# Layer 1's first projections moved into the last batch of layer 0, in a kernel of two attention layers

## The chip, the cores and the metric

The kernel runs on one core of a Trainium2 chip. The metric is the device time of one execution in microseconds (us), the median of several runs; lower is better. PE is the core's matrix engine, DVE its vector engine, ACT its scalar engine, SP the engine whose queue issues nearly all DMAs here, and PSUM the small memory that PE writes its products to. SBUF is the larger memory in which tiles live, on 128 partitions.

## The reference

Two attention layers run one after the other over x of 8 batches, 512 channels and 32x32 = 1024 tokens, in float32. The parts that matter, shortened:

```python
def _gn(v, G=32, eps=1e-5):        # group norm: 16 channels x 1024 tokens to a group
    ...
x = x + _L0_conv_ref(_gn(x), ...)  # layer 0
x = x + _L1_conv_ref(_gn(x), ...)  # layer 1

# layer 0: a second group norm, then 8 heads of 64 channels
qkv = einsum('oc,bct->bot', qkv_w, normed) + qkv_b
weight = softmax(einsum('bct,bcs->bts', q, k))
a = einsum('bts,bcs->bct', weight, v)
out = einsum('oc,bct->bot', proj_w, xf + a) + proj_b

# layer 1: heads are mixed by an 8x8 matrix before the softmax, normed over a head's whole map after it
attn = einsum('bhdq,bhdT->bhqT', q, k) * scale
attn = softmax(einsum('gh,bhqT->bgqT', w_head, attn))
attn = (attn - mean) / sqrt(var + EPS) * in_gamma + in_beta   # per batch and head
out = einsum('bhqT,bhdT->bhqd', attn, v).reshape(b, t, c) @ w_proj.T + b_proj
```

Layer 1 of batch 0 needs layer 0 of batch 0 alone. Nothing in it needs layer 0 of batch 7.

## The kernel before, in words

The order of the instructions on each engine is the order of the program, written by hand. All eight batches go through layer 0 (`with ExitStack() as l0`, from L650), then all eight through layer 1 (`l1`, from L1149). x after layer 0 is written to DRAM (`x1_d`) and read again by layer 1. Each layer opens its own pools of SBUF and PSUM, so layer 1's tiles lie where layer 0's were.

**A projection** of 512x512 weights over 1024 tokens is made by seven products of half-size blocks in place of eight (a Strassen-Winograd scheme). Its left factors are seven combinations of the weights' blocks, kept in DRAM and loaded as one tile of 1.75 MB (`load_left`); its right factors are four differences of the activations' blocks, made on DVE (`combine_right`, tiles `tmp` in layer 0). In layer 0 `project0` (L860) issues the products through `product` (L856) and calls `finish` as each quarter of the output is complete; in layer 1 the class `Projection` does it in the order of `ORDER` (L1297), and `leave` takes a product out of PSUM. The order matters in that the quarter finished last frees its PSUM, and becomes readable, last. The left tiles of layer 0 have two buffers in turn (`wpool`), so a load waits for the projection two before it.

**Layer 0.** `attention0(b, agenda)` runs 64 steps i over (half of the tokens f, pair of heads hp, block of 128 keys kc), two at a time: `scores` (L982) on PE, exp on ACT (L987), and two steps later `values` (L1008) on PE and `sums` on DVE (L993, L995), which add up the exponentials in `zacc`. Eight steps make a group g. Two steps after a group, `totals` adds `zacc` over the partitions on PE by a matrix of ones (L1030, tile z), ACT and DVE copy a half of the result each (L1035, L1036), and two small DMAs bring one line of each into 128 rows (`zc`). Four steps on, `reciprocals` adds the halves of `values` on DVE, inverts zc, writes it to DRAM and reads it back spread over the partitions (`zd`, `rzb`; L1049, L1052). Four steps after that, `finish` multiplies and adds into `xa` on DVE (L1068, L1070).

An `Agenda` holds work to be issued at a given step. In all batches but the last, the next batch's statistics (`stats0`: pm at L620 at slot 43, pv at L631 at slot 45), the loads of its left factors and its normalization (slots 49 to 61) are on it, and after the attention the next batch's k is projected, then the rest of the agenda runs (the last group's totals, reciprocals and finish), then v, q, and the batch's own output projection `out0`. In the last batch nothing follows: the agenda runs, then `out0`, then `stats_out` (L646, L647) for the four channel blocks.

**Between the layers.** All group statistics of layer 1 are finished for all batches at once (`GroupStats`: `means`, `squares`, `root`; pm L620, pv L631, then some 20 small DVE instructions), y of batch 0 is loaded (L1251) and normalized (L1273, L1277), and k, half of v, the sums of v (L1411) and q of batch 0 are projected. wv is loaded into the second buffer of `re_t`.

**Layer 1.** `Attention1.half_step(x)` runs for 32 half steps and five more. Each makes two blocks of scores (L1575), which DVE or ACT copy into `raw` (L1588, L1590); every second half step a tile t of `raw` is complete and eight DMAs of 256 KB regroup it, one for each r, into a buffer of `re_t` (L1599), at first all at once (x up to `MLAG` = 4), later one behind each score or mix. Four half steps later `mix` (L1623) reads it, with the exponential on ACT, the sums and sums of squares on DVE, and `values` (L1669) one half step after. A mix is 64 small products and needs all eight r. `pieces` are further DMAs, one issued behind each block of scores from x = 5 on: the next batch's y and left factors of k, and, put ahead of these three times a batch, rzb, the inverse of the sums. The second half of v (`v_pair`, L1394) is made at x = 1 and x = 2; its weights lie in the first half of the buffer of `re_t` that tile t = 1 is regrouped into.

Of the kernel before, what the change touches and what calls it, by code (L numbers as in the profile page):

```python
# [18 lines left out]
P = 128  # L19
# [448 lines left out]
def tile_two_attention_layers(  # L468
# [25 lines left out]
    FB = 512  # L494
# [109 lines left out]
    class GroupStats:  # L604
# [8 lines left out]
        def tile(self, tag, bufs=None):  # L613
            return self.pool.tile([P, self.w], F32, tag=tag, name=f"{tag}_{self.nm}", bufs=bufs)
# [27 lines left out]
    def channel_stats(pool, x, mv, nm):  # L642
# [4 lines left out]
        nc.vector.bn_aggr(mv, bn.rearrange("p f s -> p (f s)"))  # L647


    with ExitStack() as l0:  # L650
# [157 lines left out]
        def normalize0(b, c):  # L808
            if c == 0:
                n_t[b] = act.tile([P, NCC, T], F32, tag="n", name=f"n_{b}")  # L810
# [89 lines left out]
        def qk0(b, which):  # L900
            tiles, o0 = (q_t, 0) if which == "q" else (k_t, 1)
            t = tiles[b] = act.tile([P, NCC, T], F32, tag=which, name=f"{which}0_{b}")
# [15 lines left out]
        def v0(b):  # L918
            t = v_t[b] = act.tile([P, NT, C], F32, tag="v", name=f"v0_{b}")
# [20 lines left out]
            project0(f"pv0_{b}", "v", n_t[b], finish, by_token=True)  # L940

# [28 lines left out]
        def attention0(b, agenda):  # L970
# [50 lines left out]
            def totals(g):  # L1021

                z = [
                    ps_a.tile([P, FB], F32, tag="a0", name=f"z_{b}_{g}", bufs=2),
                    small_psum(f"z_{b}_{g}_1"),
                ]
                for a in range(2):
                    rows = slice(a * D, a * D + D)
                    for m in range(2):
                        nc.tensor.matmul(  # L1030
                            z[a][m * D : m * D + D], ones[rows, :D], zacc[g][rows, m],
                            start=True, stop=True,
                        )
                row = zpool.tile([P, 2, FB], F32, tag="row", name=f"row0_{b}_{g}", bufs=1)
                nc.scalar.copy(row[:, 0], z[0])  # L1035
                nc.vector.tensor_copy(row[:, 1], z[1])  # L1036
                zc[g] = stat.tile([P, 2, T // P], F32, tag="zc", name=f"zc_{b}_{g}")
                for a in range(2):
                    nc.sync.dma_start(out=zc[g][:, a], in_=row[0::D, a])

            def reciprocals(g):

                nc.vector.tensor_add(u[g][0], u[g][0], u[g][1])
                zs = stat.tile([P, T // P], F32, tag="zs", name=f"zs_{b}_{g}")
                nc.vector.tensor_add(zs, zc[g][:, 0], zc[g][:, 1])
# [60 lines left out]
        for b in range(B):  # L1106
# [22 lines left out]
            else:  # L1129
                ag.at(32, lambda: load_left("p", b))  # L1130
            attention0(b, ag)
            slot = NI + 2
            if more:
                combine_right(f"{b + 1}", n_t[b + 1])
                qk0(b + 1, "k")
            ag.flush()
# [845 lines left out]
```

## Time and profile before

| What | us |
|---|---|
| median of 3 runs (4342.40 to 4345.67) | 4345.27 |
| the profiled execution, its own time | 4355.81 |
| its span, first to last instruction | 4353.9 |
| layer 0's last attention ends on PE | 1747.2 |
| first scores of layer 1 | 1869.6 |
| first scores of layer 1's second batch | 2185.5 |
| PE busy | 4192.3 |
| DVE busy | 2911.7 |
| ACT busy | 2329.9 |
| mean granted clock of PE | 0.995 |

Busy time is the union of an engine's instructions; matmuls are pipelined, so a busy PE is not PE at its peak. In a line of the timeline the numbers are the start, the length, the engine, the line of the program, the operation, what it writes and reads, the shape and the count of instructions merged; idle time ahead of it stands in brackets with what ended it. One product of float32 in the program is two matmul instructions in the trace.

### The profile page before, as it was taken

Reading aid. Unit: us, or ns where it says so; the run is one execution under the profiler, and the core shown is the slowest. Engines: PE = TensorE matmul, PEld = TensorE weight load, DVE = VectorE, ACT = ScalarE, POOL = GpSimd, SP = SyncE. Lnnn points to the kernel's source line nnn. Section 1 sums busy time; section 2 is a strip of 40 time slices with the busy share of each in tenths; the row PEclk is TensorE's granted clock in tenths of the full one; section 3 lists DMA queues with packets and bytes.
Section 4 is the critical chain, followed back from the end, with each engine's and each line's share of the span. In section 5 each row is a group of like instructions: output and inputs, shape, how many; then the busy total and the mean of one; then the engine's idle time right before and its main releaser. Section 6 shows DMA issues by size and latency. Waiting matters only on the chain.

```text
span 4353.9 us, 131477 instructions
## 1 busy us (share of the span) xinstructions
PE 4192.3 (96%) x58568; PEld 2243.2 (52%) x58568; DVE 2911.7 (67%) x3881; ACT 2329.9 (54%) x2730; POOL 53.3 (1%) x86
## 2 busy tenths in 40 slices
PE   7999999999999999799999999999999999999998
PEld 4353535353535353356466466466466466465565
DVE  4748484848484848458668668568577578577577
ACT  1717171717171716158368278277187287286385
POOL 0000000000000000000000000000000000000000
PEclk9999999999999999899999999999999999999999
DMA  4213131212121211257367377277286286375474
GB/s 145 77 54 101 50 104 49 79 49 79 52 76 54 74 49 43 87 140 191 123 166 183 105 187 180 97 195 189 81 202 172 90 206 158 114 199 141 135 175 136
DMA packets 260464, 521.21 MB, mean 120 GB/s; under 512 B 58992, under 2 KB 66544, under 8 KB 253232
## 3 DMA queue, kind: packets, MB, share of 16 engines
q1 hardware_dynamic: 255008, 509.92, 41.8%
q8 instruction: 461, 7.55, 0.8%
q0 software_dynamic: 2576, 0.69, 0.3%
q10 hardware_dynamic: 2304, 2.10, 0.2%
q14 instruction: 115, 0.94, 0.1%
HBM read 196.11 MB, written 46.92 MB: 56 GB/s over the span
## 4 chain that ended last, share of the span: by engine, by line
PE 84%; DVE 6%; DMA 5%; ACT 2%; issue 2%; SPq 1%; POOL 0%; DVEq 0%; ACTq 0%; POOLq 0%
PE a L1669 11%; PE s L1575 11%; PE m L1623 10%; PE s L982 8%; PE a L1008 8%; PE pk L1319 5%; PE pq L1319 4%; PE pp_p L856 4%; PE pv_p L856 4%; PE pv L1394 4%; PE pk_p L856 4%; PE pq_p L856 4%; PE pp L1319 3%; DMA re<-raw 2%; PE t L1700 2%
## 5 line engine op out<-in xcount | busy, mean ns | idle before, releaser
L1623 PEld LDWEIGHTS m<-wmix,re 64*64 64x64 f32 x32768 | 585.4, 135 | 141.9 <-issue 73.7
L1623 PE MATMUL m<-wmix,re 64*64 64x64 f32 x32768 | 602.1, 219 | 44.0 <-issue 34.9
L987 ACT ACTIVATE e<-s 128x1024 f32<-128x1024 f32 x512 | 497.4, 1026 | 235.4 <-PE s L982 235.4
L1629 ACT ACTIVATE e<-m 128x1024 f32<-128x1024 f32 x512 | 528.2, 1032 | 157.7 <-PE m L1623 154.2
L1647 DVE TENSOR_TENSOR z<-z,e 128x1024 f32<-128x1024 f32 x448 | 538.9, 1218 | 69.8 <-ACT e L1629 69.6
L1651 DVE TENSOR_TENSOR z<-z,e 128x1024 f32<-128x1024 f32 x448 | 534.9, 1219 | 74.6 <-ACT e L1640 74.4
L1669 PE MATMUL a<-e,v 128*64 128x256 f32 x4096 | 558.2, 392 | 27.5 <-ACT q L1691 20.9
L1575 PE MATMUL s<-k,q 64*64 64x256 f32 x8192 | 558.4, 388 | 6.2 <-DVE q L1431 4.6
L1590 ACT COPY raw<-s 128x1024 f32<-128x1024 f32 x368 | 372.7, 1015 | 284.4 <-PE s L1575 245.8
L982 PE MATMUL s<-q,k 64*64 64x512 f32 x4096 | 491.5, 594 | 2.3 <-ACT e L987 2.3
L995 DVE TENSOR_TENSOR zacc<-zacc,e 128x1024 f32<-128x1024 f32 x384 | 468.2, 1219 | 28.6 <-ACT e L987 3.9
L1008 PE MATMUL a<-e,v 64*64 64x512 f32 x4096 | 485.0, 589 | 0.0
L1640 ACT ACTIVATE e<-e 128x1024 f32<-128x1024 f32 x448 | 462.1, 1063 | 0.0
L1575 PEld LDWEIGHTS s<-k,q 64*64 64x64 f32 x8192 | 271.5, 132 | 274.5 <-issue 170.7
L1669 PEld LDWEIGHTS a<-e,v 128*64 128x64 f32 x4096 | 250.6, 136 | 155.0 <-issue 24.9
L1008 PEld LDWEIGHTS a<-e,v 64*64 64x64 f32 x4096 | 159.9, 133 | 281.2 <-issue 281.2
L982 PEld LDWEIGHTS s<-q,k 64*64 64x64 f32 x4096 | 156.2, 133 | 281.5 <-issue 257.7
L1588 DVE COPY raw<-s 128x1024 f32<-128x1024 f32 x144 | 176.1, 1223 | 96.3 <-PE s L1575 84.7
L1394 PE MATMUL pv<-re,y 128*128 128x512 f32 x512 | 227.6, 598 | 0.0
L1394 PEld LDWEIGHTS pv<-re,y 128*128 128x128 f32 x512 | 94.8, 190 | 120.1 <-issue 120.1
L1399 DVE COPY v<-pv 128x512 f32<-128x512 f32 x32 | 22.1, 689 | 149.4 <-ACT v L1398 149.4
L856 PE MATMUL pv_p<-left_v,tmp 128*128 128x256 f32 x512 | 115.1, 383 | 4.2 <-DVE tmp L885 4.2
(285 smaller groups left out, 4133.0 us busy)
## 6 DMA issues: line engine op xcount, KB each, us to landing
re<-raw SPq DMA_DIRECT2D x1024, 256.0 KB
left_q<-left_q SPq DMA_DIRECT2D x17, 1792.0 KB
left_p<-left_p SPq DMA_DIRECT2D x17, 1792.0 KB
left_k<-left_k SPq DMA_DIRECT2D x10, 1792.0 KB
x<-in_x_dram SPq DMA_DIRECT2D x32, 512.0 KB
rzb<-zd SPq DMA_DIRECT2D x128, 128.0 KB
x<-x SPq DMA_DIRECT2D x64, 256.0 KB
rzb<-zd SPq DMA_DIRECT2D x64, 256.0 KB
```

The costliest lines, as they stand in the source:

```text
L856: nc.tensor.matmul(out, st, mv, start=start, stop=(k == 1), skip_group_check=True)
L982: nc.tensor.matmul(ps[c * D : c * D + D, m], k[r, hp, k0 : k0 + D], q[r, hp, ts(f, FB)], start=True, stop=True,)
L987: nc.scalar.activation(e[i], ps, AF.Exp, scale=S0 * S0)
L1008: nc.tensor.matmul(acc[g][a][m * D : m * D + D], v[rows, kc, ts(2 * hp + m, D)], e[i][rows, m], start=(kc == 0), stop=(kc == NG - 1),)
L1319: nc.tensor.matmul(self.ps[m][:, i], w[:, left, k * HC + i * P : k * HC + i * P + P], right[:, k], start=(k == 0 and m != 2), stop=(k == 1 ...
L1394: nc.tensor.matmul(ps[:, m], y_t[b][:, c, ts(2 * i + m, P)], w[:, c], start=(c == 0), stop=(c == NCC - 1),)
L1575: last = nc.tensor.matmul(pv[c * D : c * D + D, m, j], qo_t[b][r, 2 * qb + j, hp, ts(c, D)], k_t[b][r, hp, ts(kb, KB)], start=True, stop=True,
L1623: last = nc.tensor.matmul(ps[c * D : c * D + D, a, ts(r, D)], self.re[t, r][rows, j, k0 : k0 + D], wmix[rows].rearrange("p g i -> p (g i)" ...
L1629: nc.scalar.activation(self.e[y][:, j], ps.rearrange("p a c -> p (a c)"), AF.Exp)
L1647: nc.vector.tensor_add(self.z[:, j], self.z[:, j], self.e[y][:, j])
L1651: nc.vector.tensor_add(self.z2[:, j], self.z2[:, j], self.e2[j])
L1669: last = nc.tensor.matmul(self.acc[w][two * D : two * D + D, s].rearrange("p (c i) -> p c i", i=Q8), v_t[b][:, kc, ts(g, D)], e[:, g], sta ...
```

## The change

Six things are changed. (1) The tiles n, q, k and v of both layers come from one pool, `shared`, that stays open over both. (2) In layer 0's last batch, y of layer 1's batch 0 is loaded at slot 20, the group statistics of batches 0 to 6 are finished at slots 22, 25 and 28, the left factors of layer 1's k and q are loaded at 32 and 33 (before: those of `out0` at 32), and y is normalized at 49 to 61; after the attention come layer 1's k, the rest of the agenda, the load for `out0`, layer 1's q, the load of wv, `out0`, and then the first two pairs of v with `stats_out` between them. These use layer 0's `project0`. (3) In layer 1's first batch the statistics of batch 7 alone are finished at half steps 0, 1 and 2. (4) `totals` makes one z in four products of 128 rows, 32 columns of ones and 256 elements, ACT alone copies it, and one DMA makes zc; the addition of two halves on DVE is gone. (5) `ORDER` ends with 3, 4 for 4, 3. (6) The second v pair of a layer 1 batch is made in half step 3, after its scores and mix and ahead of its regrouping; tile t = 1 is regrouped in the order 4 to 7, 0 to 3; and rzb is spread by four DMAs of 32 partitions in place of two of 64.

```diff
+    shared = both.enter_context(tc.tile_pool(name="shared", bufs=1))
+    gstat = both.enter_context(tc.tile_pool(name="gstat", bufs=1))
+    def group_stages(b0, b1, psum):
+        gs = GroupStats(
+            gstat, psum, mvs[:, b0:b1].rearrange("p b c s -> p (b c) s"), f"1_{b0}", keep=1
+        )
+        def end():
+            gs.root()
+            at = slice(b0 * NCC, b1 * NCC)
+            nc.vector.tensor_copy(gmean[:, at], gs.gm)
+            nc.vector.tensor_copy(grstd[:, at], gs.r1)
+            nc.vector.scalar_tensor_tensor(
+                gneg[:, at], gs.gm, -1.0, gs.r1, ALU.mult, ALU.mult
+            )
+            nc.vector.scalar_tensor_tensor(
+                ys[:, b0:b1].rearrange("p b c -> p (b c)"), gs.dm, float(T), gs.r1,
+                ALU.mult, ALU.mult,
+            )
+        return gs.means, gs.squares, end
+    def normalize_to(y, b, c):
+        i = b * NCC + c
+        if c % 2:
+            nc.scalar.activation(
+                y, y, AF.Identity, bias=gneg[:, i : i + 1], scale=grstd[:, i : i + 1]
+            )
+        else:
+            nc.vector.tensor_scalar(
+                y, y, gmean[:, i : i + 1], grstd[:, i : i + 1], ALU.subtract, ALU.mult
+            )
...
-                n_t[b] = act.tile([P, NCC, T], F32, tag="n", name=f"n_{b}")
+                n_t[b] = shared.tile([P, NCC, T], F32, tag="n", name=f"n_{b}")
...
-            t = tiles[b] = act.tile([P, NCC, T], F32, tag=which, name=f"{which}0_{b}")
+            t = tiles[b] = shared.tile([P, NCC, T], F32, tag=which, name=f"{which}0_{b}")
...
-            t = v_t[b] = act.tile([P, NT, C], F32, tag="v", name=f"v0_{b}")
+            t = v_t[b] = shared.tile([P, NT, C], F32, tag="v", name=f"v0_{b}")
...
+        def bank(x, m):
+            return x[m] if isinstance(x, list) else x[:, m]
+        def first_k1():
+            t = k_t["1"] = shared.tile([P, NCC, T], F32, tag="k", name="k1_0")
+            def finish(i, j, x, y):
+                for m in range(2):
+                    dst = t[:, 2 * i + m, ts(j, FB)]
+                    if y is None:
+                        nc.scalar.copy(dst, x[m])
+                    else:
+                        nc.vector.tensor_add(dst, bank(x, m), y[:, m])
+            project0("pk1_0", "k1", n_t["1"], finish)
+        def first_q1():
+            t = q_t["1"] = shared.tile([P, NT, NCC, P], F32, tag="q", name="q1_0")
+            def view(a):
+                return a.rearrange("p (r i j) -> p j i r", r=NR, i=Q8)
+            def finish(i, j, x, y):
+                for m in range(2):
+                    dst = t[:, :, 2 * i + m, ts(j, D)].rearrange("p j (i r) -> p j i r", r=NR)
+                    if y is None:
+                        nc.scalar.copy(dst, view(x[m]))
+                    else:
+                        nc.vector.tensor_add(dst, view(bank(x, m)), view(y[:, m]))
+            project0("pq1_0", "q1", n_t["1"], finish)
+        def first_wv():
+            w = left_tile("v1", 0).rearrange("p f k o -> p (f k o)")[:, : NCC * C]
+            left_t["v1"] = w.rearrange("p (c o) -> p c o", c=NCC)
+            for c in range(NCC):
+                nc.sync.dma_start(out=left_t["v1"][:, c], in_=wvT[ts(c, P)])
+        def first_v1(i):
+            if i == 0:
+                v_t["1"] = shared.tile([P, NT, C], F32, tag="v", name="v1_0")
+            ps = score_psum(f"pv1_0_{i}")
+            for m in range(2):
+                for c in range(NCC):
+                    nc.tensor.matmul(
+                        ps[:, m], n_t["1"][:, c, ts(2 * i + m, P)], left_t["v1"][:, c],
+                        start=(c == 0), stop=(c == NCC - 1),
+                    )
+            nc.scalar.copy(v_t["1"][:, 2 * i], ps[:, 0])
+            nc.vector.tensor_copy(v_t["1"][:, 2 * i + 1], ps[:, 1])
...
             def totals(g):
-                z = [
-                    ps_a.tile([P, FB], F32, tag="a0", name=f"z_{b}_{g}", bufs=2),
-                    small_psum(f"z_{b}_{g}_1"),
-                ]
-                for a in range(2):
-                    rows = slice(a * D, a * D + D)
-                    for m in range(2):
-                        nc.tensor.matmul(
-                            z[a][m * D : m * D + D], ones[rows, :D], zacc[g][rows, m],
-                            start=True, stop=True,
-                        )
-                row = zpool.tile([P, 2, FB], F32, tag="row", name=f"row0_{b}_{g}", bufs=1)
-                nc.scalar.copy(row[:, 0], z[0])
-                nc.vector.tensor_copy(row[:, 1], z[1])
-                zc[g] = stat.tile([P, 2, T // P], F32, tag="zc", name=f"zc_{b}_{g}")
-                for a in range(2):
-                    nc.sync.dma_start(out=zc[g][:, a], in_=row[0::D, a])
+                HB = FB // 2
+                z = ps_a.tile([P, FB], F32, tag="a0", name=f"z_{b}_{g}", bufs=2)[:, :HB]
+                for c in range(4):
+                    nc.tensor.matmul(
+                        z[c * 32 : c * 32 + 32], ones[:, :32], zacc[g][:, c // 2, ts(c % 2, HB)],
+                        start=True, stop=True, tile_position=(0, c * 32),
+                    )
+                row = zpool.tile([P, HB], F32, tag="row", name=f"row0_{b}_{g}")
+                nc.scalar.copy(row, z)
+                zc[g] = stat.tile([P, T // P], F32, tag="zc", name=f"zc_{b}_{g}")
+                nc.sync.dma_start(out=zc[g], in_=row[0::32])
             def reciprocals(g):
                 nc.vector.tensor_add(u[g][0], u[g][0], u[g][1])
-                zs = stat.tile([P, T // P], F32, tag="zs", name=f"zs_{b}_{g}")
-                nc.vector.tensor_add(zs, zc[g][:, 0], zc[g][:, 1])
+                zs = zc[g]
...
             else:
-                ag.at(32, lambda: load_left("p", b))
+                def load_first():
+                    t = n_t["1"] = shared.tile([P, NCC, T], F32, tag="n", name="y_0")
+                    for c in range(NCC):
+                        nc.sync.dma_start(out=t[:, c], in_=x1_d[0][ts(c, P), :])
+                ag.at(20, load_first)
+                for slot, fn in zip((22, 25, 28), group_stages(0, B - 1, small_psum)):
+                    ag.at(slot, fn)
+                ag.at(32, lambda: load_left("k1", 0))
+                ag.at(33, lambda: load_left("q1", 0))
+                for c in range(NCC):
+                    ag.at(49 + 4 * c, lambda c=c: normalize_to(n_t["1"][:, c], 0, c))
             attention0(b, ag)
             slot = NI + 2
             if more:
                 combine_right(f"{b + 1}", n_t[b + 1])
                 qk0(b + 1, "k")
+            else:
+                combine_right("y1", n_t["1"])
+                first_k1()
             ag.flush()
             if more:
                 load_left("q", b + 1)
                 v0(b + 1)
                 load_left("p", b)
                 qk0(b + 1, "q")
+            else:
+                load_left("p", b)
+                first_q1()
+                first_wv()
             combine_right(f"{b}_xa", xa_t[b])
             out0(b)
             tmp.clear()
-        for c in range(NCC):
-            stats_out(B - 1, c)
+        for i in range(2):
+            first_v1(i)
+            for c in range(2 * i, 2 * i + 2):
+                stats_out(B - 1, c)
...
-        ypool = l1.enter_context(tc.tile_pool(name="ypool", bufs=1))
-        qopool = l1.enter_context(tc.tile_pool(name="qopool", bufs=1))
-        kvpool = l1.enter_context(tc.tile_pool(name="kvpool", bufs=1))
...
-        y_t, qo_t, k_t, v_t, w_t = {}, {}, {}, {}, {}
+        y_t, qo_t, k_t, v_t = ({0: t["1"]} for t in (n_t, q_t, k_t, v_t))
+        w_t = {}
...
-                y_t[b] = ypool.tile([P, NCC, T], F32, tag="y", name=f"y_{b}")
+                y_t[b] = shared.tile([P, NCC, T], F32, tag="n", name=f"y_{b}")
...
-        def load_y(b, chunks=range(NCC)):
...
-        gs.means()
-        gs.squares()
-        gs.root()
-        gneg = const_tile("gneg", [P, B * NCC])
-        nc.vector.scalar_tensor_tensor(gneg, gs.gm, -1.0, gs.r1, ALU.mult, ALU.mult)
...
+        def normalize1(b, c):
+            normalize_to(y_t[b][:, c], b, c)
...
         class Projection:
-            ORDER = (1, 6, 2, 7, 5, 4, 3)
+            ORDER = (1, 6, 2, 7, 5, 3, 4)
...
                     self.piece(last)
                 if x % 2 and i == 1:
-                    self.due = [(t, r) for r in R_ORDER]
+                    order = (4, 5, 6, 7, 0, 1, 2, 3) if t == 1 else R_ORDER
+                    self.due = [(t, r) for r in order]
                 if x % 2 == 0 and i == 0:
...
                 rzb = self.rzb
                 spread = [
-                    lambda two=two: nc.sync.dma_start(
-                        out=rzb[two * D : two * D + D], in_=zd[two].partition_broadcast(D)
+                    lambda i=i: nc.sync.dma_start(
+                        out=rzb[ts(i, 32)], in_=zd[i // 2].partition_broadcast(32)
                     )
-                    for two in range(2)
+                    for i in range(4)
                 ]
                 if ag is None:
...
+                ag.run(x - 0.75)
                 if x <= MLAG or x >= NX:
                     self.regroup(n=NR)
...
-        load_left(("k", 0))
-        load_y(0)
         load_w(("v", 0), wvT, re_t[:, 1, : NCC * C])
-        normalize1(0)
-        right_tile(0)
-        right_y(0)
-        k_projection(0).run()
-        load_left(("q", 0))
-        v_pair(0, 0)
-        v_pair(0, 1)
-        v_sums()
-        q_projection(0).run()
         NV = NT // 4
         for b in range(B):
             more = b + 1 < B
             a = Attention1(b)
             ag = Agenda()
-            for i in range(NV):
-                ag.at(1 + i, lambda i=i: v_pair(b, NV + i))
+            for i, slot in enumerate((1, 3 - 0.75)):
+                ag.at(slot, lambda i=i: v_pair(b, NV + i))
+            if b == 0:
+                for x, fn in enumerate(group_stages(B - 1, B, small_psum1)):
+                    ag.at(x, fn)
+                ag.at(3 - 0.75, v_sums)
...
```

## The prediction

> **What bounds the kernel now.** I read the page first (busy time, slices, clock), then the list of PE's waits, then the timelines of the places where PE waits.
>
> ```profile
> PE 4192.3 (96%) x58568; PEld 2243.2 (52%) x58568; DVE 2911.7 (67%) x3881; ACT 2329.9 (54%) x2730; POOL 53.3 (1%) x86
> PEclk9999999999999999899999999999999999999999
> ```
>
> PE is busy for 96% of the span, so a gain can only come from less PE work or from PE's idle time (some 137 us when the pieces between matmuls are added up, much of it tenths of a microsecond in layer 1). The clock line has one slice below 9, the 17th (1741 to 1850 us), which holds the seam between the layers. The view by stages and PE's timeline show that seam:
>
> ```profile
> 1747.20:1756.70 9.50, 8.15 (x24) 3.17 (x24) 4.39 (x11) 2.83 (x5) 0.00 (x0) 1.00 0.13 31
> 1756.70:1780.30 23.60, 16.15 (x34) 7.10 (x34) 9.78 (x10) 1.01 (x1) 0.00 (x0) 0.86 0.09 33
> 1780.30:1800.90 20.60, 4.81 (x13) 2.31 (x11) 17.92 (x45) 0.51 (x1) 0.00 (x0) 0.72 0.73 254
> 1800.90:1827.90 27.00, 27.00 (x57) 11.94 (x58) 11.46 (x10) 4.00 (x4) 0.00 (x0) 0.90 0.13 50
> ```
> ```profile
> 1748.55 1.09 PE L1030 MATMUL z<-zacc,ones 64*64 64x512 f32 x8 [1.35 <-DVE zacc L995]
> 1764.16 12.84 PE L856 MATMUL pp_p<-tmp_xa,left_p 128*128 128x512 f32 x24 [7.45 <-DVE tmp_xa L836]
> ...
> 1794.28 0.61 PE L620 MATMUL pm<-gs_m,gavg 128*128 128x32 f32 x2 [10.41 <-DVE gs_m L618]
> 1795.85 0.64 PE L631 MATMUL pv<-gs_sq,gavg 128*128 128x32 f32 x2 [0.96 <-DVE gs_sq L629]
> 1800.90 6.38 PE L1319 MATMUL pk<-y,left_k 128*128 128x512 f32 x8 [4.41 <-DMA y<-x]
> ```
>
> Columns of a stage: its length, busy time of PE, PEld, DVE, ACT, POOL, then granted clock, DMA share, GB/s. PE waits 24.6 us here (1.35 + 7.45 + 10.41 + 0.96 + 4.41): for the last group's division, for the norm's statistics, for y. Some work after the waits runs at half clock: the first 8 pk take 6.38 us, another 8 take 3.60. From the clock's records 4.6 us of pp and 5.4 us of pk lie at 0.5, so about 5.0 us are lost besides. The seam costs 29.6 us.
>
> Inside the stages PE is back to back, and three more places matter: the totals of layer 0, with the statistics that follow some of them, and the start of each layer 1 batch.
>
> ```profile
> 1722.99 1.04 PE L1030 MATMUL z<-zacc,ones 64*64 64x512 f32 x8
> 1723.85 1.90 PE L982 MATMUL s<-q,k 64*64 64x512 f32 x16
> ```
> ```profile
> 1948.22 1.08 PE L1669 MATMUL a<-e,v 128*64 128x256 f32 x8
> 1949.23 1.92 PE L1700 MATMUL t<-z,ones 128*32 128x512 f32 x16
> 1951.09 1.09 PE L1575 MATMUL s<-k,q 64*64 64x256 f32 x16
> ```
> ```profile
> 400.77 0.69 DVE L1068 TENSOR_TENSOR u<-u,rzb 128x512 f32<-128x512 f32 x1 [1.24 <-DMA rzb<-zd]
> ...
> 402.11 0.68 DVE L1036 COPY row<-z 128x512 f32<-128x512 f32 x1
> 402.71 0.16 DVE L618 COPY gs_m<-mv 128x4 f32<-128x4 f32 x1
> 403.02 0.36 PE L620 MATMUL pm<-gs_m,gavg 128*128 128x4 f32 x2 [2.04 <-DVE gs_m L618]
> ```
> ```profile
> 1907.01 0.56 PE L1623 MATMUL m<-wmix,re 64*64 64x64 f32 x19 [2.31 <-issue]
> 2222.43 0.34 PE L1623 MATMUL m<-wmix,re 64*64 64x64 f32 x8 [0.83 <-DMA re<-raw]
> ```
>
> **The change, part by part.** All sums are made against the profiled execution: span 4353.9, its own time 4355.8, which is 10.5 above the median of 4345.27. I subtract from the median.
>
> *A, the totals (64 of them).* Old: from z's start to the next s 0.86 us for 8 instructions of 512 columns, 0.1075 each with four tiles at work at once. New: 8 instructions of 256 columns in 128x32 tiles, which nothing in layer 0 uses; the nearest row is layer 1's t, the same tile shape: 1.86 us for 16 of 512 columns (1949.23 to 1951.09) against 16 x 0.1075 = 1.72, so four column tiles do overlap, and 0.14 is for leaving the shape; the a before it takes 1.01 where 0.86 would be its share, so 0.15 for entering. New total: 8 x 0.054 + 0.29 = 0.72, 0.14 less for the 56 inside an attention (8), and up to 0.43 less for the 8 that stand between 128x128 projections, where the shape changes anyway (3.5). A = -12. Bounds: no price for the shape, -27; a fixed price per instruction as in t (0.116 x 8 + 0.14 = 1.07), +13. The old copy of half the row on DVE, the addition and one of the two zc DMAs go at no cost on the path.
>
> The Trainium skill speaks against A: "TensorEngine Tiling (Array Packing)", Tiling Modes, Key Properties, says that changing the tile mode, not just the tile, drains the engine. The rows agree in kind. That page has no price; with the 166 ns constant of a warm matmul in "TensorE: Matmul & The Clock Gate", Single matmul latency, paid twice, z would be 0.76 by an estimate and A -9.
>
> *A', the statistics behind a total.* In seven batches pm waits for DVE, 10.9 us together (1.0 to 2.55 each, at about 184, 401, 621, 839, 1056, 1273 and 1490 us). The wait is z, then the row copy on DVE, then gs_m. The copy moves to ACT alone, so gs_m need not wait for z: some 0.7 of each, 5 us. Where the division before it waits for rzb (as at 400.77) the rest stays. After 403 and 1492 a clock of 0.5 stands for 3.4 us, 1.7 lost each; I count half of one. A' = -6, bounds 0 and -14 (10.9 + 3.4).
>
> *B, the seam.* Removed: 29.6 us. k1's 24 us hide the last group's division, as k's do in the other batches (there PE waits 0.3 between k, z and v); out0's weights load behind q1 (24 us) and wv behind out0 (24 us), both after a PE wait on SP as in the other batches. What comes back: (1) q1 leaves by DVE additions with a strided view, 1.06 us each at L1431 against 0.75 at L912. Four stand before the two that free the accumulators out0 needs, so out0 starts some 1.8 us after q1 instead of 0.2. (2) The last batch's statistics now stand on DVE behind v's second copy: v ends at 13.7 us after out0 (32 x 0.43), copies to 15.1, two statistics of 1.42 to 17.9, the raw copy 1.22 to 19.1, gs_m 19.35. PE has done two scores by 15.5 and then stands at pm: 3.9 us. (3) pv stands behind the copy of v pair 2 on DVE: 0.6 + 0.7 + 0.9 = 2.2 us. (4) One score 0.4; two more pm and pv 1.1; a half-clock window after the 3.9 us wait, 1.7 (gaps of 4.17 and 4.19 stand in the trace, one with a 3.4 us window at 0.5 after it). (5) In the last attention SP gets y (2 MB, 8.3 us at the 254 GB/s above) at slot 20, ahead of zd and rzb of a group divided at slot 26; DVE may stand a few us there, with sums queued behind it. DVE is busy 96.2 of 116.7 us, and PE meets it only at z and at free e tiles. 1 us, and 1 for pm and pv. Together 0.3 + 1.8 + 3.9 + 2.2 + 0.4 + 1.1 + 1.7 + 2 = 13.4; B = -16. Bounds: (2) as long as the old 10.4 with its clock, -8; nothing comes back but 0.3 and 1.8, -27.
>
> The skill's "TensorE: Matmul & The Clock Gate", What's actually happening, has the half clock after one idle window of about 3.4 us; here it came 5.2 us into the 7.45 us gap (1756.7 to 1761.95). By the page the 3.9 us wait is long enough; by that row it would not be, and B would be -18.
>
> *C, the start of a layer 1 batch.* Regrouping the second tile (8 DMAs of 256 KB) starts after its copies and PE needs it some 5 to 10 us later; m waits 3.1 us in batch 0 (0.77 + 2.31) and 1.5 to 2.8 in the others, 13.6 more, 16.7 in all, on re or on "issue" while the DMA engines are full. The second v pair (7 us of PE, wv in the first half of that buffer) now stands after these scores; four regroups go to the other half under it, and four wait on SP for its end, with 10 us of PE work still ahead of their use. The first tile keeps its cover. C = -10; bounds 0 and -16.7.
>
> *D, the order 3, 4.* The first score waits 0.57 eight times (4.6) for q's last addition. With 4 last, scores 0 and 1 are free, but the third takes that accumulator, 0.45 later. D = -1, bounds 0 and -4.6.
>
> *E, rzb in four DMAs of 128 KB for two of 256.* Each goes behind a score, two per half step, so the burst spreads over two. m's waits in the half steps after it sum to about 23 us over layer 1, mostly "issue". A sixth of it, -4; bounds +4 (14 more issues on SP behind which regroups stand) and -15.
>
> Sum: -12 - 6 - 16 - 10 - 1 - 4 = -49; 4345.3 - 49 = 4296.
>
> **The rivals.**
> 1. *The DMA waits stay* (C and E nothing): "issue" is the releaser of 34.9 of m's 44.0 us, and the bytes to regroup are the same. Against it: the worst waits stand where eight regroups are in flight. 4296 + 14 = 4310.
> 2. *The tile shape eats A* (0 to +13): 4308 to 4321. For it, the 0.29 above; against it, t's 16 in 1.86.
> 3. *The seam's wait moves rather than goes*: pm stands on DVE's tail as gs_m did. Against it, 14 us of v now lie before it. B = -8: 4304.
> 4. *Slower*: the four 128x32 products don't overlap in layer 0. Each instruction then takes 0.215, z 1.72 + 0.29 = 2.0, 1.14 more than now, +73 where I have -12: 4381. The other parts give 37, so it decides from a z of 0.86 + 37/64 = 1.44 us. Nothing in the profile speaks for it but that the shape is new there; t speaks against it.
> 5. *The clean case*: A -20, B -20, C -14, E -8 and A' -8: 4274.
>
> **How the numbers follow.** Forecast 0.52 (4285 to 4303 by itself), rival 1 0.18, rival 2 0.12, rival 3 0.08, rival 4 0.04, rival 5 0.06. The range, 4266 to 4321, holds all but rival 4 and the tails of the others. A run tells 0.2% (8.7 us) from no change: faster 0.93, same 0.03, slower 0.04.
>
> **What would show it.** z to the next s about 0.72 (1.44 or more is rival 4); the seam's waits of 7.45 and 10.41 gone, a wait of some 4 us at pm of the last batch, 1.8 ahead of out0; no clock below 9 in the 17th slice, or only just; m's waits in the first four half steps of a batch under 1 us. The forecast is wrong if pm's wait is near 10 us, or if layer 1's batches, 315 us apart now, have not shrunk.

## The result and the profile after

The changed kernel takes 4272.51 us (median of 4 runs, 4269.45 to 4273.32) beside 4344.50 before (4 runs, 4342.40 to 4345.67): 72 us less, a ratio of 0.9834 [0.9816, 0.9851]. The profiled executions stand further apart, 4267.5 against 4353.9 us of span, because the one of before was 10.5 us above its median and the one of the changed kernel 3 us below its own.

The page of the changed kernel: busy times, the clock by slices, and the group of the mixes (busy time and mean ns, then the idle time ahead of them).

```profile
PE 4158.3 (97%) x58572; PEld 2213.3 (52%) x58572; DVE 2862.8 (67%) x3780; ACT 2319.2 (54%) x2735; POOL 53.3 (1%) x86
PEclk9999999999999999999999999999999999999999
L1706 PE MATMUL m<-wmix,re 64*64 64x64 f32 x32768 | 591.0, 219 | 22.4 <-issue 19.7
```

PE is still the bound. Its idle time between matmuls, pieces added up, fell from 137.0 to 84.8 us, its busy time by 34 us; every slice of the clock is at 9. The same group of before had 602.1 and 44.0, so 21.6 us of waits left the mixes of layer 1.

PE's timeline through the seam, by start and length, with the idle time ahead in brackets:

```profile
1747.87 7.13 PE L903 MATMUL pq_p<-y,left_q 128*128 128x512 f32 x16 [0.21 <-DVE k L1002]
...
1773.91 7.13 PE L903 MATMUL pp_p<-xa,left_p 128*128 128x512 f32 x16 [1.73 <-DVE q L1019]
...
1798.04 13.90 PE L1036 MATMUL pv<-left_v,y 128*128 128x512 f32 x32
...
1813.34 1.96 PE L1656 MATMUL s<-k,q 64*64 64x256 f32 x32 [1.40 <-DVE v L1041]
...
1817.66 0.38 PE L622 MATMUL pm<-gs_m,gavg 128*128 128x4 f32 x2 [2.36 <-DVE gs_m L620]
...
1830.80 0.36 PE L633 MATMUL pv<-gs_sq,gavg 128*128 128x4 f32 x2 [2.15 <-DVE gs_sq L631]
...
1833.52 1.96 PE L1656 MATMUL s<-k,q 64*64 64x256 f32 x32 [0.48 <-DVE raw L1671]
```

The waits of 7.45, 10.41 and 4.41 us are gone. What came back is 0.21, 1.73, 3.76 (1.40 for v's copy and 2.36 for the statistics), 2.15 and 0.48 us: 8.3 where 24.6 stood. The fall of the idle time is thus found: 21.6 us at the mixes, 16.3 here, 10.5 at pm (below) and 2.0 at q make 50.4 of the 52. The stages of the changed kernel around the waits (length, busy time of PE, PEld, DVE, ACT, POOL, then granted clock, DMA share, GB/s):

```profile
1819.00:1822.40 3.40, 3.40 (x22) 1.45 (x15) 1.22 (x1) 1.01 (x1) 0.00 (x0) 0.50 0.00 0
...
1846.30:1849.70 3.40, 3.40 (x84) 2.67 (x84) 0.22 (x1) 1.01 (x1) 0.00 (x0) 0.50 0.68 143
```

Two windows of 3.4 us run at half clock, so 3.4 us are lost where the forecast counted 5.0 for the old seam.

Next, one total inside layer 0's attention, in PE's timeline of before and then of the changed kernel:

```profile
212.48 1.90 PE L1008 MATMUL a<-e,v 64*64 64x512 f32 x16
214.20 1.04 PE L1030 MATMUL z<-zacc,ones 64*64 64x512 f32 x8
215.06 1.90 PE L982 MATMUL s<-q,k 64*64 64x512 f32 x16
216.77 1.90 PE L1008 MATMUL a<-e,v 64*64 64x512 f32 x16
```
```profile
209.65 1.90 PE L1109 MATMUL a<-e,v 64*64 64x512 f32 x16
211.48 0.64 PE L1128 MATMUL z<-zacc,ones 128*32 128x256 f32 x8
212.05 1.95 PE L1083 MATMUL s<-q,k 64*64 64x512 f32 x16
213.82 1.90 PE L1109 MATMUL a<-e,v 64*64 64x512 f32 x16
```

From z to the next s are 0.86 and 0.57 us. That alone misleads: the a before the new z takes 1.83 instead of 1.72 until the z starts, and the s after it 1.77 instead of 1.71. From a to a it is 4.29 and 4.17 (means of 49 places 4.292 and 4.163), so a total inside the attention saves 0.13 us. The time between first scores of two batches of layer 0 nevertheless fell from 216.9 to 219.6 us down to 214.5 to 215.0. The rest is at the seven totals with a pm behind them. The DVE's timeline around the second of these, in the changed kernel, shows what became of their wait (z starts at 396.23):

```profile
394.84 0.69 DVE L1163 TENSOR_TENSOR u<-u,rzb 128x512 f32<-128x512 f32 x1 [1.18 <-DMA rzb<-zd]
395.57 0.69 DVE L1165 TENSOR_TENSOR xa<-xa,u 128x512 f32<-128x512 f32 x1
396.18 0.16 DVE L620 COPY gs_m<-mv 128x4 f32<-128x4 f32 x1
```

In before, DVE started that u 0.86 us after z, behind the same wait for rzb, and then the row copy; now it starts 1.4 us ahead of z, and no copy stands before gs_m. Six of the seven waits of pm are gone and one of 0.42 is left. The chain from a z to its rzb has shrunk: from z's start to the reciprocal on DVE are 9.4 us in before and 6.7 now (means of the seven places). Of the 2.7 us, 1.0 is the issue of the last zc DMA (3.15 and 2.15 us after z's start); 1.7 lie between that issue and the reciprocal, where now one transfer has to land instead of two and the addition is missing.

### The profile page after: what moved, and what is told of

The parts are those of the page before. It is cut to its first block, busy times and chain, and to the rows that moved or that the text cites. A ratio compares the mean times of both kernels' runs of the same rounds, so it can differ in the third digit from the quotient of the medians.

```text
span 4267.5 us, 131379 instructions
## 1 busy us (share of the span) xinstructions
PE 4158.3 (97%) x58572; PEld 2213.3 (52%) x58572; DVE 2862.8 (67%) x3780; ACT 2319.2 (54%) x2735; POOL 53.3 (1%) x86
## 4 chain that ended last, share of the span: by engine, by line
PE 90%; DVE 4%; ACT 2%; DMA 2%; issue 1%; SPq 0%; POOL 0%; DVEq 0%; ACTq 0%; POOLq 0%
PE a L1752 11%; PE s L1656 11%; PE m L1706 11%; PE s L1083 10%; PE a L1109 10%; PE pp_p L903 5%; PE pk_p L903 5%; PE pq_p L903 4%; PE pv_p L903 4%; PE pk L1400 4%; PE pq L1400 4%; PE pv L1475 4%; PE pp L1400 3%; PE t L1783 2%; ACT q L1774 1%
## 5 line engine op out<-in xcount | busy, mean ns | idle before, releaser
L1706 PE MATMUL m<-wmix,re 64*64 64x64 f32 x32768 | 591.0, 219 | 22.4 <-issue 19.7
L1475 PE MATMUL pv<-re,y 128*128 128x512 f32 x480 | 214.5, 600 | 0.0
```

Source lines behind the costliest of these rows:

```text
L1475: nc.tensor.matmul(ps[:, m], y_t[b][:, c, ts(2 * i + m, P)], w[:, c], start=(c == 0), stop=(c == NCC - 1),)
L1706: last = nc.tensor.matmul(ps[c * D : c * D + D, a, ts(r, D)], self.re[t, r][rows, j, k0 : k0 + D], wmix[rows].rearrange("p g i -> p (g i)" ...
```

## The experiments

Each kernel is the changed one with the edit shown, timed in five rounds beside the kernel before. The changed kernel ran in each of three groups, as the zero of its group, and differences are between medians within a group. Three executions of the unmodified changed kernel also show how far the waits of m scatter.

**The changed kernel again**, three times, with no edit.

> The changed kernel once more, as the reference point of the next three. Theory: 0.983 of the kernel before, some 4272 us; z to the next s 0.57 us; m's waits near 22 us. If the 72 us are partly a slow day of the kernel before (its profiled execution lay 10.5 above its own median), the ratio is nearer to 0.987 here.

> The changed kernel as the reference point of the next three: 0.983 of the kernel before.

> The changed kernel beside the next three: 4270 to 4280 us, ratio 0.982 to 0.9855; the waits of m 20 to 28 us in all, 4 to 5 of them in half steps 4 to 7.

4275.19, 4278.21 and 4273.34 us; ratios 0.9832 [0.9819, 0.9846], 0.9835 [0.9818, 0.9851] and 0.9832 [0.9818, 0.9845]. The kernel before took 4351.07, 4353.93 and 4347.22 us beside them, so the whole change is worth 74 to 76 us there, and the 72 are no slow day of the kernel before. m waits 20.0, 28.4 and 22.2 us in their profiles; in half steps 4 to 7 alone, over all batches, 4.3, 7.1 and 3.8, after 4.7 in the first profile. So a difference of some 5 us in time, or of 8 us in m's waits, says little by itself.

**A and A' undone**: the old totals. With them z takes the small PSUM buffer that the statistics need, so in the last batch these are issued three slots earlier.

```diff
-                HB = FB // 2
-                z = ps_a.tile([P, FB], F32, tag="a0", name=f"z_{b}_{g}", bufs=2)[:, :HB]
...
+                z = [
+                    ps_a.tile([P, FB], F32, tag="a0", name=f"z_{b}_{g}", bufs=2),
+                    small_psum(f"z_{b}_{g}_1"),
+                ]
...
-                for slot, fn in zip((22, 25, 28), group_stages(0, B - 1, small_psum)):
+                for slot, fn in zip((19, 22, 25), group_stages(0, B - 1, small_psum)):
```

> The changed kernel with the old totals (two z of 64x64 tiles, half the row copied by DVE, two zc DMAs and their addition); the three stages of the statistics stand at slots 19, 22 and 25 so that z finds its PSUM free. Theory 'z costs 0.57 for 0.86, and pm no longer waits for DVE's copy': 64 x 0.29 = 18.6 back, and 8 to 10 us of waits at pm with one or two half-clock windows (1.7 each), 27 to 32 us above the changed kernel, 4300 to 4304. Rival 'the sizes of the prediction' (A 12 and A' 6): 18 above, 4290. Rival 'the z alone': 18.6 above with pm's waits staying away.

4301.56 us, 26.4 more; 0.9889 [0.9874, 0.9904]. From the list of PE's waits (us in total, times, the longest), the line of pm in before, in the changed kernel as first profiled, and in this one:

```profile
PE pm L620 <- DVE gs_m L618: 21.3, 8, 10.4
PE pm L622 <- DVE gs_m L620: 2.8, 2, 2.4
PE pm L622 <- DVE gs_m L620: 13.5, 9, 2.5
```

Less the seam's 10.4, 2.4 and 2.4, and less 1.0 at a place that the earlier slots bring in the last batch, these are 10.9, 0.4 and 10.1 us. The waits behind the totals are back, and so is a window at half clock after 403 us. Undoing the totals costs 26 us, of which 1 belongs to the earlier slots: just under the band expected and half as much again as the forecast's 18.

**The copy on DVE**: the new total, but DVE copies its row.

```diff
-                nc.scalar.copy(row, z)
+                nc.vector.tensor_copy(row, z)
```

> The changed kernel with the copy of the row of totals on DVE instead of ACT (half the elements of the old copies). Theory 'pm waited because gs_m stood behind a copy on DVE that waits for z': pm's waits return in the seven batches, 0.7 to 1 us each, 5 to 8 us above the changed kernel with one half-clock window perhaps. Rival 'pm waited for rzb, which now comes sooner because zc takes one DMA': no wait at pm, no difference in time.

4283.12 us (4274.40 to 4286.32), 4.9 more, 0.9836 [0.9820, 0.9852]: within the scatter, so its time settles nothing. The trace does. DVE's timeline at the same total, and PE's waits for gs_m:

```profile
397.80 0.69 DVE L1163 TENSOR_TENSOR u<-u,rzb 128x512 f32<-128x512 f32 x1 [1.41 <-DMA rzb<-zd]
398.53 0.69 DVE L1165 TENSOR_TENSOR xa<-xa,u 128x512 f32<-128x512 f32 x1
399.66 0.42 DVE L1133 COPY row<-z 128x256 f32<-128x256 f32 x1 [0.43 <-PE z L1128]
400.00 0.16 DVE L620 COPY gs_m<-mv 128x4 f32<-128x4 f32 x1
```
```profile
PE pm L622 <- DVE gs_m L620: 8.3, 8, 2.4
```

DVE is free 0.43 us before z has come, waits, copies, and only then makes gs_m. Less the 2.4 of the seam, pm waits 5.9 us in seven places, where before had 10.9 and the changed kernel has 0.4. So about half of A' is the copy off DVE. The other half is the division that is over before z: PE's products, the copy, the single DMA and the missing addition all lie ahead of rzb. The times given with the result put most of it on the zc DMAs and the addition; no run takes them one by one.

**B undone**: the seam of before with the rest of the change.

```diff
-    shared = both.enter_context(tc.tile_pool(name="shared", bufs=1))
-    gstat = both.enter_context(tc.tile_pool(name="gstat", bufs=1))
...
-            else:
-                combine_right("y1", n_t["1"])
-                first_k1()
...
+        load_left(("k", 0))
+        load_y(0)
         load_w(("v", 0), wvT, re_t[:, 1, : NCC * C])
+        normalize1(0)
...
+        k_projection(0).run()
...
```

> The kernel before with the new totals, the order 3, 4, the later second v pair with its regrouping order, and rzb in four DMAs; the seam between the layers as it was (part B alone undone). Theory 'B is the waits and the half clock of the seam, less what comes back': the traces have 24.6 us of waits and 5.0 of half clock before, and after it 8.3 us of waits (0.21, 1.73, 1.40, 2.36, 2.15, 0.48), 3.4 of half clock and about 1 of further work; so 17 us above the changed kernel, about 4289 where that is 4272. Rival 'the moved work hides nothing else and costs the last attention its own slack': 10 above or less. Rival 'the seam is worth all 29.6': 30 above.

4290.43 us, 12.2 more; 0.9862 [0.9845, 0.9878]. PE's timeline in its seam:

```profile
1736.38 13.05 PE L856 MATMUL pp_p<-tmp_xa,left_p 128*128 128x512 f32 x24 [4.12 <-DVE tmp_xa L836]
...
1766.71 0.61 PE L620 MATMUL pm<-gs_m,gavg 128*128 128x32 f32 x2 [10.42 <-DVE gs_m L618]
...
1773.42 6.43 PE L1312 MATMUL pk<-y,left_k 128*128 128x512 f32 x8 [4.51 <-DMA y<-x]
```

Two of the three long waits are as before. The first is 4.12 for 7.45: the shorter total gets the last group's division done earlier in the old seam too, so 3.3 us of the forecast's B belong to A as well and are counted only once in the sum.

**C undone**, both halves of it.

```diff
-                    order = (4, 5, 6, 7, 0, 1, 2, 3) if t == 1 else R_ORDER
+                    order = R_ORDER
...
-            for i, slot in enumerate((1, 3 - 0.75)):
+            for i, slot in enumerate((1, 2)):
```

> The changed kernel with the second v pair at half step 2 again, ahead of scores 3, and tile t = 1 regrouped in the old order (part C undone). m's waits in half steps 4 to 7 were 14.8 us before and are 4.7 after. Theory: they are back, some 10 us above the changed kernel (4282). Rival 'the new order of pools and the seam took these waits': no difference.

4288.06 us, 12.9 more; 0.9855 [0.9839, 0.9870]. m's waits in half steps 4 to 7, over all batches, are 11.0 us (14.8 before, 4.3 in the changed kernel of the group). That is some 7 of the 12.9 us. From the seam on this profile also has 20.5 us at half clock, 10.2 more than that of the changed kernel in the group, which is another 5 us; how much of that belongs to the edit is not shown. The list of PE's waits, of the changed kernel as first profiled and of this one, has the share with a transfer named:

```profile
PE m L1706 <- DMA re<-raw: 2.2, 5, 0.7
```
```profile
PE m L1706 <- DMA re<-raw: 7.0, 12, 0.9
```

**C by halves**: first the old order behind the later v pair (only the first line above), then the new order with the pair at half step 2 (only the second).

> The v pair stays in half step 3, but its tile is regrouped in the old order, whose first DMA goes to the half in which the weights of v lie. Theory (place and order need each other: that DMA stands on SP until the pair's last product, and the other seven behind it): all of what part C is worth is lost, 10 to 16 us over the changed kernel, m's waits in half steps 4 to 7 at 10 us or more. Rival (the cover by the later pair is what counts, the order nothing): 0 to 4 us over it, waits there near 5 us.

> The new order of the regrouping stays, the v pair is back in half step 2. With the pair over, both halves of the buffer are free and the order can do nothing. Theory (the cover by the later pair is what counts): as with both undone, 10 to 14 us over the changed kernel, m's waits in half steps 4 to 7 near 11 us. Rival (the mix needs the second half of r first, so the order alone helps): 3 to 8 us over it, waits there 6 to 8 us.

Old order, late pair: 4279.17 us, 5.8 more, 0.9852 [0.9837, 0.9867]; m's waits in half steps 4 to 7 are 9.6 us (3.8 in the changed kernel of the group, 7.1 at most in any execution of it). New order, early pair: 4295.24 us (4288.42 to 4299.20), 21.9 more, 0.9887 [0.9872, 0.9902]; waits there 14.2. Of the four pairings (early or late pair, old or new order) the costs over the changed kernel are thus 12.9, 21.9, 5.8 and 0. None of the expectations met both: with the late pair the old order loses part of the gain, not all, and its 5.8 us are hardly clear of the scatter; with the early pair the new order is worse than the old one by 9 us. The intervals of these two just miss each other, but their executions overlap (4284.73 to 4292.04 and 4288.42 to 4299.20), and m's waits in these half steps differ by 3.2 us only. The later pair is the main thing, and the order gained nothing without it. Whether and why it harms there stays open.

**D undone**.

```diff
-            ORDER = (1, 6, 2, 7, 5, 3, 4)
+            ORDER = (1, 6, 2, 7, 5, 4, 3)
```

> Part D undone, layer 1's products in the order 4, 3 again. Theory of the forecast: 1 us over the changed kernel, inside the scatter; the first score of a batch waits 0.57 us on DVE seven times (4.0 in all) where the changed kernel has 2.6 (0.37 at the third). Rival (the order costs rather than gives): faster by 2 us or more.

4280.62 us (4277.03 to 4288.10), 7.3 more; 0.9851 [0.9837, 0.9864], an interval that overlaps that of the changed kernel a little. PE's waits for q's last addition, in this kernel and in the changed one of the group:

```profile
PE s L1656 <- DVE q L1512: 4.0, 7, 0.6
```
```profile
PE s L1656 <- DVE q L1512: 2.5, 7, 0.4
```

The step itself is 1.5 us, as forecast. The other 6 are not in it: m waits 30.1 us here against 22.2, 4.1 of the difference in half steps 8 to 11 and 3.7 in 16 to 19, and against the 28.4 of another execution of the changed kernel that is little. Whether the order has an indirect effect stays open.

**E undone**: rzb in two DMAs.

```diff
-                        out=rzb[ts(i, 32)], in_=zd[i // 2].partition_broadcast(32)
+                        out=rzb[two * D : two * D + D], in_=zd[two].partition_broadcast(D)
```

> The changed kernel with rzb spread by two DMAs of 64 partitions again (part E undone). In the two traces m's waits in half steps 16 to 19 and 24 to 27 fell from 17.4 to 6.2 us. Theory 'the burst of two 256 KB transfers starves PE': these waits are back, m waits about 33 us and the time is 9 to 13 us above the changed kernel (4282 to 4285). Rival 'the prediction's size' (E = -4): 4 us above. Rival 'the waits differ from run to run and the DMAs have no part in it': no difference.

4284.07 us, 8.9 more; 0.9849 [0.9835, 0.9862]. m waits 29.5 us against 20.0. In half steps 16 to 19 and 24 to 27, where rzb is spread, it is 6.4 and 3.7 against 3.3 and 1.1; before had 9.5 and 7.9, and the kernels that keep the four DMAs have 4.1 to 9.0 in the two together, beside 10.1 here. So E removes part of those waits, more than the forecast took. But most of that fall is there without E too, and the total scatters by as much between executions of the changed kernel itself, so 9 us is a measured time whose mechanism the traces support only in part.

**What is left in the seam**: statistics of all four blocks ahead of v's copies, gs_m before the last of them, pm right behind v's products and its squares during the first scores, pv and the root before the second v pair; v's second pair in two PSUM buffers of layer 0, and q's quarter (1,1) finished after (1,0), so that `out0` finds its accumulators free. Layer 1 also opens its two PSUM pools in the other order.

```diff
-        for i in range(2):
-            first_v1(i)
-            for c in range(2 * i, 2 * i + 2):
-                stats_out(B - 1, c)
+        for c in range(NCC):
+            stats_out(B - 1, c)
+        last_gs = GroupStats(
+            gstat, small_psum, mvs[:, B - 1 : B].rearrange("p b c s -> p (b c) s"),
+            f"1_{B - 1}", keep=1,
+        )
+        first_v1(0)
+        first_v1(1, last_gs.means)
+        last_gs.squares_dve()
...
-                for x, fn in enumerate(group_stages(B - 1, B, small_psum1)):
-                    ag.at(x, fn)
+                last_gs.psum = small_psum1
+                ag.at(1, last_gs.squares_pe)
+                ag.at(1, group_stages(B - 1, B, None, last_gs)[2])
...
-            project0("pq1_0", "q1", n_t["1"], finish)
+            project0("pq1_0", "q1", n_t["1"], finish, late=True)
```

> A candidate: the four stats_out ahead of both v copies on DVE, batch 7's gs_m ahead of the second copy and its pm right after v's second pair, pv after scores 0 and 1, the second v pair of layer 0's end in the other PSUM buffers, and q1's quarter (1,1) added after (1,0), so that out0 finds its accumulators 0.9 us sooner. Theory 'the waits that came back (1.40, 2.36, 2.15, 0.48 and half of 1.73) are due to the order on DVE, and the two half-clock windows to them': they go, 8 to 10 us below the changed kernel (4263). Rival 'DVE has as much to do there in any order, and the wait shows up a few instructions later': within 3 us of it.

4267.71 us (4263.85 to 4268.02), 10.5 less than the changed kernel of its group (4272.42 to 4283.74); 0.9806 [0.9792, 0.9820] of before. PE's timeline in its seam:

```profile
1773.95 7.05 PE L909 MATMUL pp_p<-xa,left_p 128*128 128x512 f32 x16
...
1811.73 0.28 PE L622 MATMUL pm<-gs_m,gavg 128*128 128x4 f32 x2
1812.84 3.68 PE L1678 MATMUL s<-k,q 64*64 64x256 f32 x64 [0.82 <-DVE gs_gm L626]
```

No wait is left ahead of `out0` or pm, and 0.82 us stand ahead of the scores. This is the fastest of all kernels run, and it shows that the waits that came back were still on the path: waits of 1.73, 3.76, 2.15 and 0.48 fell to 0.82 and 0.16, 7.1 us of the 10.5. Of the rest little is named: m waits 25.4 us for 28.4, which is inside the scatter, and this kernel has one window at half clock in its seam, but so had the execution of the changed kernel that was profiled beside it.

## Why the prediction was right, and where its sum was short

The direction, the places and the bound were right, and 4272.5 lies in the range. It does not lie in the forecast's own band of 4285 to 4303: the sum of -49 was 23 us short, because A' and E were put at half or less of what they gave, and C and D came out higher too. The range held because it took in the clean case, which had a chance of 0.06. Undone one at a time, the parts are worth 26.4 + 12.2 + 12.9 + 7.3 + 8.9 = 67.7 us, where the whole is 72 by the first timing and 74 to 76 in the groups in which they were undone.

*A, the totals.* Right in mechanism and price. The new z was put at 0.72 us with the price of its shape; from a to a it is 0.86 - 0.13 = 0.73, of which 0.11 for entering, 0.57, and 0.06 for leaving. The sign that the forecast named, z to the next s at 0.72, was looked for at the wrong place: entering the shape lengthens the a ahead of it. At the batch ends 1.02 became 0.71, 0.31 each for the 0.43 allowed. In all 49 x 0.13 + 7 x 0.31 = 8.5 us. At the seven with a pm behind them, the stretch from the a ahead of z to the s behind pm lost 12.8 us together, 10.5 of them waits, so 2.3 for the shape: 10.8 for 12. The rule on mode switches in the Trainium skill's "TensorEngine Tiling (Array Packing)" (Tiling Modes, Key Properties) thus shows as 0.17 us in and out together besides what lies in z itself; whether that is a drain no row shows. The estimate of 0.76 from the constant in "TensorE: Matmul & The Clock Gate" (Single matmul latency) was nearly as good as 0.72.

*A', the waits of pm.* Mis-sized: -6, where the lower bound of -14 was what happened. Two sentences of the step failed. "Where the division before it waits for rzb (as at 400.77) the rest stays": it did not, because the totals' own change brings rzb earlier, from 0.86 us after z to 1.4 before it. Half of one window at half clock was counted; those after 403 and 1492 us both went. 10.9 - 0.4 = 10.5 us of waits and 3.4 of clock make 13.9, and with A's 10.8 that is 24.7 of the 26.4 measured by undoing both (there the window after 403 came back and that after 1492 did not). What lies behind the first: the chain from z to rzb was costed at nothing since it is off the path, though the prediction's own rows showed DVE waiting for its end.

*B, the seam.* Right. Its five waits were put at 0.3, 1.8, 3.9, 2.2 and 0.4 us and measured 0.21, 1.73, 3.76, 2.15 and 0.48. The places are as named but for one: 1.40 of the 3.76 stand ahead of the first scores, for v's copy, and only 2.36 at pm. The half-clock loss was 3.4 for 1.7 in this profile, and 1.7 to 5.1 in the others of the same kernel. Undoing B costs 12.2, and 3.3 of its first wait fall to A; together 15.5 for the 16. On the clock, the row and the page were weighed on a wait of 3.9 us in one piece; it came as 1.40 and 2.36 with scores between, and the half clock came at 1819.0, right after. By "TensorE: Matmul & The Clock Gate" (What's actually happening) in the Trainium skill an idle window of about 3.4 us is needed; no wait here was that long, and the half clock came all the same. The measurement decides: in the 3.41 us ahead of it PE was busy for 1.31 us (last section).

*C, the start of a batch.* Right in kind, -10 for 12.9. m's waits in half steps 4 to 7 fell from 14.8 to 4.7 us (the 16.7 that the forecast counted there are 14.8 in the profile), and to under 1 us a batch in six of the eight. The reason given for it, four regroups under the pair and four behind it, is borne out in part: the pair's place without the order keeps about half of the gain, the order without the place brings none.

*D.* -1; the wait itself moved by 1.5 to 2.0. The time of 7.3 is larger and not explained.

*E, rzb in four.* Mis-sized: "a sixth" of 23 us was taken, -4, and 8.9 measured. The waits in the half steps that follow the spreading (16 to 19 and 24 to 27) fell from 17.4 to 6.2 us, but with E undone they are 10.1, so 7 of these 11 us are not E's; the upper bound of +4 for more issues on SP did not show.

Together C, D and E were put at 15 us and give 29, the largest shortfall. How much of it belongs to which is less sure: D and E alone are not far above the scatter of their timing. The sum is seen in the batches of layer 1: the six between the first and the last took 314.8 to 320.4 us from first scores to first scores, and now take 310.4 to 312.1 (309.2 to 315.2 in the three repetitions).

*The rivals.* That the transfers' waits stay is refuted by the mixes' 44.0 to 22.4. That the tile shape eats A, or that its products don't overlap, is refuted by z's 0.57 (1.44 was the point of decision). That the seam's wait moves was right for 3.76 us and no more. The clean case came nearest, at 4274, and in part by luck: its C of -14 and E of -8 are close to what was measured, but its A and B of -20 each were not reached, and its A' of -8 was too small.

## What to carry to other kernels

A chain that lies off the path of the bounding engine still has a price if an in-order engine waits at its end with other work queued behind it: cost the whole chain, from first product to last use, before saying what stays. Small waits of the bounding engine, counted by place and over all batches, can be worth more than the one large hole that one sees first: here C, D and E gave 29 us when undone one at a time, the seam 12. When work is moved over a seam, look at what its copies and statistics stand behind on the slower engine, for that order, with the choice of PSUM buffers, was worth another 10 us.

## What the chip showed that was not expected

Windows of half clock lie on a grid: within an execution their starts are whole numbers of steps of 3.413 us apart. In before they start at 68.9, 403.4, 1492.3, 1762.0 and 1789.3, with 98, 319, 79 and 8 steps between them. With seams that wait alike, four executions of the changed kernel had windows at 1819.0 and 1846.3, at 1818.7 (two steps long) and 1849.4, at 1831.2 only, and at 1822.0 and 1849.3. What decides is how a wait falls into the cells of the grid. The same wait of 2.36 us for pm lies, but for 0.26 us, in one cell in the changed kernel as first profiled (first two lines), and across a line of the grid in its second repetition (the next three). In each line PE's busy time is the first number behind the length, and the granted clock the third from the end:

```profile
1815.56:1818.97 3.41, 1.31 (x22) 1.04 (x26) 1.82 (x4) 1.01 (x1) 0.00 (x0) 1.00 0.32 118
1818.97:1822.38 3.41, 3.41 (x22) 1.48 (x15) 1.22 (x1) 1.01 (x1) 0.00 (x0) 0.50 0.00 0
```
```profile
1814.13:1817.54 3.41, 1.96 (x32) 1.13 (x32) 3.15 (x8) 0.30 (x1) 0.00 (x0) 1.00 0.83 259
1817.54:1820.95 3.41, 2.08 (x34) 1.42 (x34) 1.88 (x3) 0.71 (x1) 0.00 (x0) 1.00 0.15 56
1820.95:1824.36 3.41, 2.93 (x11) 1.30 (x8) 0.62 (x1) 1.01 (x1) 0.00 (x0) 1.00 0.25 51
```

A cell with 1.31 us of work is followed by half clock, cells with 1.96 and 2.08 are not. So it is in all 14 traces of this case. Of the cells at full clock (after the first 100 us), all 31 in which PE was busy for 40% or less were followed by a window of half clock, 10 of the 15 between 40 and 48%, and only 7 of the some 17,000 busier ones. Those 7 all lie over the sums of v, in layer 1's first batch:

```profile
1842.47 3.90 PE L1492 MATMUL pvs<-ys,re 128*64 128x8 f32 x128
```

PE counts as busy there, with 128 instructions of 8 columns each. In six of the 7 cells they fill 87% or more of the cell, and the seventh is idle where they do not fill it; in six other traces they fill 76% of a cell at most, and no window follows. The second window in the stages of the changed kernel (1846.3) is such a one, and so is that of the last kernel of the seam, at 1838.9, with no wait over 0.82 us in the 100 us before it. So a wait of 2 us near a seam costs 1.7 us more or not, as it falls in the grid; and since the same waits had windows in different places in the four executions above, which it will be is not known beforehand.
